# Row 0 five weight groups ahead of row 1 instead of four, 40 attention pieces beside row 1's units, SBUF tiles at 2 KB boundaries

## The chip, the cores and the metric

The kernel runs on one core of a Trainium2 chip. A core has five engines that run beside each other, each through its own list of instructions in order: TensorE (PE, matrix products), VectorE (DVE), ScalarE (ACT), GpSimd (POOL) and SyncE (SP, which here issues all transfers). They meet at semaphores. SBUF is the on-chip memory, 128 partitions wide; products land in PSUM. The metric is the device time of one launch in microseconds (us); lower is better.

## The reference

Two transformer layers on an input of 2 rows x 512 positions x 512 channels. Each layer has an attention and a feed-forward part, each behind a layer norm with shift, scale and gate that come from a conditioning vector per row:

```python
sa, ca, ga, sb, cb, gb = (silu(c) @ wmod) ...      # per row of the batch
x = x + ga * L0_attn(layernorm(x) * (1 + ca) + sa)
x = x + gb * L0_ffn(layernorm(x) * (1 + cb) + sb)   # weights reduced to their sign
x = x + ga' * L1_attn(layernorm(x) * (1 + ca') + sa')
x = x + gb' * L1_ffn(layernorm(x) * (1 + cb') + sb')
```

- Layer 0's attention is a gated linear recurrence: 32 heads of 128 channels, 8 key/value groups of 4 heads, computed in 4 chunks of 128 positions with a state carried from chunk to chunk, a decay per head, an RMS norm, a gate and an output projection.
- Layer 0's feed-forward is one 512 x 512 product with sign weights.
- Layer 1's attention is softmax attention with 32 heads of 16 channels over 512 positions of a row.
- Layer 1's feed-forward mixes 4 streams of 128 channels; the 4 x 4 mixing matrix of each position comes from 50 Sinkhorn iterations, a long chain of tiny operations.

The two rows of the batch do not depend on each other anywhere.

## The kernel before

**Units of layer 0.** The work of layer 0's attention is cut into *steps*, one for each pair of a weight group (0 to 7) and a row (0 or 1), and each step into 4 *units*, one for each chunk of 128 positions: 16 steps, 64 units. `AHEAD` sets the order of the steps. The first `8 - AHEAD` groups are done for row 0 and row 1 by turns, so that the weights of a group are loaded once for both rows; then row 0 does its last `AHEAD` groups alone, and then row 1 does its own. The weights of these last groups are loaded twice, once for each row. With `AHEAD = 4`, units 0 to 31 alternate, units 32 to 47 are row 0's, units 48 to 63 are row 1's.

```python
    steps = [(g, b) for g in range(KV0 - AHEAD) for b in range(B)]
    steps += [(g, b) for b in range(B) for g in range(KV0 - AHEAD, KV0)]
```

A group of weights is 14 tiles of 128 x 512 numbers (256 KB): 1 for the keys, 4 for the queries, 1 for the values, 4 for the gate, 4 for the output. Each is loaded by SyncE (`raw_tile`, line 200), split into a high part by ACT (line 209) and a low part by POOL (line 210), since each product is made of three passes over such parts (`passes`, line 232). The loop over units (from line 1374) issues, beside the unit's own work, the projections and the loads of the next steps.

A unit has the scores (`scores`, decays loaded as `gb` at line 493), the state, `mix` (its first products into `yps`, line 548, are used here as the start of a unit), the turn of its result and the output projection into `x` (`project_out`).

**The tail of a row.** `tail(n)` is called after unit n. For each row it runs, chunk by chunk over the next units, the layer norm, the feed-forward of layer 0 (products at line 629), the second layer norm, and at last the projections of layer 1's keys, values and queries. `ends` says at which unit a row's tail begins: the second chunk of its last step, 45 for row 0 and 61 for row 1. The projections follow 8 units later, at unit 53 for row 0. They go through a bias on ACT (line 661), a rotation on VectorE and POOL (lines 668 to 671), a split (lines 673 and 675), are stored to DRAM (line 678) and loaded again in another shape (lines 797 and 808), all through SyncE's one queue.

**Pieces of layer 1's attention.** The softmax attention is cut into 128 *pieces*, 64 for each row. `piece()` issues, for piece p, two score tiles of 128 x 512 (product at line 842) with their maxima on VectorE (line 846), and, ten pieces later, the transposed scores (line 876) with the exponentials on ACT; every fourth piece also the output of one set of heads (line 896). Pieces begin beside row 1's units: from unit `FIRST` on, `PER = 3` pieces are issued after each unit, up to `HOLD` pieces in all:

```python
        while n >= FIRST and at[0] < min(HOLD, (n - FIRST + 1) * PER):
            piece()
```

With `FIRST = 53` and `HOLD = 33` these are 33 pieces over units 53 to 63. After the last unit the rest follow. The steps of row 1's tail that are still open then (12 virtual units) are taken one per piece from piece `HOLD` on; row 1's own pieces are 64 to 127. The Sinkhorn chains are put beside the pieces (`aside`), row 0's on POOL for the most part, row 1's on VectorE; the last one remains alone at the end.

**What sets the order.** The program is traced in the order of these calls, and a scheduler then orders each engine's instructions by priorities and its own view of when data is there; `gated` and `behind` add order-only links so that side work keeps its place. The tile pools share one SBUF space: each tile gets its address after scheduling, wherever it fits among the tiles that live at the same time. Before the change most 2 KB tiles start 128, 640 or 1,152 bytes past a 2 KB boundary.

Of the kernel before, what the change touches and what calls it, by code (L numbers as in the profile page):

```python
# [12 lines left out]
PT, OUT = 16, 1  # L13
S1, S2, MT, OT, OP = 3, 3, 2, 2, 2
QS = 6
HOLD = 33
UPS = 400, 400, 400, 400
RATES = None, None, None, None
HEAD = 16
# [4 lines left out]
HL, RA, ZL, XC, XP = 0, 0, 100, 100, 1  # L24
UPO = 600
SPLIT0, SPLIT1 = 16, 16
AHEAD = 4
FIRST = 53
PER = 3
LATE, LATE1 = 2, 12  # L30
LAG = 10
# [21 lines left out]
def tile_adaln(ctx: ExitStack, tc: tile.TileContext, a: dict, out: bass.AP):  # L53
    nc = tc.nc
    ck = ctx.enter_context(tc.tile_pool(name="ck", bufs=1))
    raws = ctx.enter_context(tc.tile_pool(name="raw", bufs=RAW))
    wts = ctx.enter_context(tc.tile_pool(name="w", bufs=1))
    small = ctx.enter_context(tc.tile_pool(name="small", bufs=4))
    wk = ctx.enter_context(tc.tile_pool(name="wk", bufs=2))
    dram = ctx.enter_context(tc.tile_pool(name="dram", bufs=1, space=bass.MemoryType.DRAM))  # L60
    psp = ctx.enter_context(tc.tile_pool(name="ps", bufs=2, space=PSUM))


    table = nc.scalar.preload_act_table_set("natural_log_exp_and_others")
# [583 lines left out]
    def load_rope1():  # L648
        l1c["rope"] = [temp([P, L], FP, f"rope1{k}", 1) for k in range(2)]
        for k in range(2):  # L650
            nc.sync.dma_start(out=l1c["rope"][k], in_=a["c_rope1"][:, k * L:(k + 1) * L])
        if "bias" not in l1c:
            l1c["bias"] = keep([P, 6])
            nc.sync.dma_start(out=l1c["bias"], in_=a["bias1"])
# [33 lines left out]

    ends = [(KV0 - AHEAD) * B * NC + AHEAD * NC - NC + 1, KV0 * B * NC - NC + 1]

    def tail(n):

        if n % 8 in (3, 4, 5, 6) and n < 40:
            mod_piece(load=n % 8 < 6)

        for b in range(B):
            c = n - ends[b]
            with behind():
                if -3 <= c < 1:
                    load_ffn(c + 3)  # L700
                    if c == -2:
                        load_ffn_rows(b)
                elif c == 5:
                    load_l1(b)
                elif 6 <= c < 8:
                    load_l1q(2 * c - 12)
                    load_l1q(2 * c - 11)
                    if c == 7:
                        load_rope1()
                if n == FIRST - 1:  # L710
                    layer1_keys()
            if 0 <= c < NC:
                l1c["a", c] = norm(x[b * NC + c])
            if 1 <= c < NC + 1:
                modulated(b, c - 1, l1c["a", c - 1], modT[0], 2, also=sum_h)
                l1c["sums", c - 1] = l1c["sum"]
            if 2 <= c < NC + 2:
                feed_forward(b, c - 2)
            if 3 <= c < NC + 3:
                l1c["b", c - 3] = norm(x[b * NC + c - 3])  # L720
            if 4 <= c < NC + 4:
                modulated(b, c - 4, l1c["b", c - 4], modT[1], 0)
            if c == 8:
                l1c["there", b] = True
                project_kv(b)
                project_q(b, 0)
                project_q(b, 1)
                project_q(b, 2)
                project_q(b, 3)
# [10 lines left out]
    def layer1_keys(js=(0, 1)):  # L740
        for s in range(2):
            empty = temp([P, L], FR, "hi1")
            nc.scalar.copy(empty, raw_tile(a["c_keys1"][s]))
            for j in js:
                ksd[j, s] = temp([P, L], FR, f"ks{j}{s}")
                nc.sync.dma_start(out=ksd[j, s].bitcast(FP), in_=empty.bitcast(FP))

    steps = [(g, b) for g in range(KV0 - AHEAD) for b in range(B)]
    steps += [(g, b) for b in range(B) for g in range(KV0 - AHEAD, KV0)]
    units = [{"at": (g, b, c)} for g, b in steps for c in range(NC)]  # L750
# [534 lines left out]
    def slack(p):  # L1285

        return LAG0 if p < HOLD else min(LAG, LAG0 + p - HOLD)

    def piece():
        p = at[0]  # L1290
        at[0] += 1
        if p == 0:
            begin()
        i, k = divmod(p, 8)
        if k == 0 and i < len(order):
            load_step(i + 1)
        if p < n_pieces:
            maxima(order[i], k)
        if wt[0] <= p - slack(p):
            weighed()  # L1300
        if k == 4 and i + 1 < len(order):
            keys1(i + 1)
        with tc.high_priority(UP):
            if p >= HOLD and p % POP == 0 and virtual:
                tail(virtual.pop(0))
        aside(2)
# [67 lines left out]
    for n, u in enumerate(units):  # L1374
# [39 lines left out]
        with extra(n):  # L1414
            tail(n)
        while n >= FIRST and at[0] < min(HOLD, (n - FIRST + 1) * PER):
            piece()
# [86 lines left out]
```

## Time and profile before

| | |
|---|---|
| median of 3 runs | 1406.62 us (1404.83 to 1407.78) |
| the profiled execution | 1401.8 us, span 1400.0 us |
| busy, TensorE / VectorE / ACT / POOL | 1245.7 / 1159.8 / 831.5 / 775.8 us |
| mean granted TensorE clock | 0.948 |
| read from HBM / written | 102.11 / 10.64 MB |
| unit 0, unit 63 (first product into `yps`) | 87.9 us, 1015.8 us |
| first score tile of row 0, of row 1 | 897.1 us, 1129.2 us |
| last transposed scores | 1270.2 us |

The span is the time from the first to the last instruction; the profiled execution's own time is 1.8 us more. Busy time of an engine counts its instructions, not its waits. A line such as `a:b d, PE busy (x) ...` gives, for the stretch from a to b, its length, and for each engine the busy time and the number of instructions, then the granted share of TensorE's clock, the share of time the transfer engines were busy and the bytes they moved.

Four phases can be told apart: the start up to about 100 us, layer 0's attention of both rows up to about 1020 us (in its last third row 0's tail and the first pieces run beside it), the pieces up to 1272 us, and the rest of row 1's Sinkhorn chain and mixing up to 1400 us.

### The profile page before, as it was taken

Reading aid. Unit: us, or ns where it says so; the run is one execution under the profiler, and the core shown is the slowest. Engines: PE = TensorE matmul, PEld = TensorE weight load, DVE = VectorE, ACT = ScalarE, POOL = GpSimd, SP = SyncE. Lnnn points to the kernel's source line nnn. Section 1 sums busy time; section 2 is a strip of 40 time slices with the busy share of each in tenths; the row PEclk is TensorE's granted clock in tenths of the full one; section 3 lists DMA queues with packets and bytes.
Section 4 is the critical chain, followed back from the end, with each engine's and each line's share of the span. In section 5 each row is a group of like instructions: output and inputs, shape, how many; then the busy total and the mean of one; then the engine's idle time right before and its main releaser. Section 6 shows DMA issues by size and latency. Waiting matters only on the chain. (4 is left out here: it accounts for less than half of the span.)

```text
span 1400.0 us, 22901 instructions
## 1 busy us (share of the span) xinstructions
PE 1245.7 (89%) x7168; PEld 992.1 (71%) x7168; DVE 1159.8 (83%) x2969; ACT 831.5 (59%) x2354; POOL 775.8 (55%) x1169
## 2 busy tenths in 40 slices
PE   5979999999999999999988999799999889994128
PEld 3758888788788778888866777577676666663117
DVE  7998668687677687787899977688799979898887
ACT  5457576476376466666665656557567467664128
POOL 4454374364264367577777748545242655558861
PEclk9989999999999999999999999999999999997568
DMA  8022241231142343324333317523203231200001
GB/s 256 23 65 60 88 121 30 68 107 53 53 118 57 92 120 106 98 68 124 118 114 91 98 53 241 170 67 91 90 24 113 71 111 52 59 11 1 1 16 46
DMA packets 95377, 117.13 MB, mean 84 GB/s; under 512 B 10828, under 2 KB 50508, under 8 KB 95256
## 3 DMA queue, kind: packets, MB, share of 16 engines
q1 hardware_dynamic: 95256, 115.67, 27.7%
q8 instruction: 57, 0.93, 0.3%
q14 instruction: 64, 0.52, 0.1%
HBM read 102.11 MB, written 10.64 MB: 81 GB/s over the span
## 5 line engine op out<-in xcount | busy, mean ns | idle before, releaser
L846 DVE TENSOR_REDUCE m<-s 128x1 f32<-128x512 f32 x256 | 166.4, 673 | 18.6 <-PE s L842 18.3
L67 ACT ACTIVATE pt<-s 128x512 f32<-128x512 f32 x256 | 136.9, 602 | 33.3 <-PE s L876 31.7
L447 POOL TENSOR_TENSOR q<-xcos,rot 128x512 f32<-128x512 f32 x64 | 92.8, 1450 | 61.6 <-DVE xcos L445 57.1
L67 ACT ACTIVATE sg<-sg 128x512 f32<-128x512 f32 x128 | 80.6, 632 | 68.5 <-DVE sg L478 66.8
L876 PE MATMUL s<-qs,ks 100*128 100x256 f32 x512 | 103.3, 306 | 11.0 <-DMA qs<-mm 7.4
L842 PE MATMUL s<-ks,qs 96*128 96x512 f32 x256 | 103.6, 437 | 9.7 <-DVE m L846 7.5
L515 POOL TENSOR_TENSOR gb<-gb,q 128x512 f32<-128x512 f32 x48 | 63.2, 1319 | 77.7 <-ACT gb L67 68.7
L232 PE MATMUL pps<-hh,wq_h 128*128 128x512 f32 x256 | 103.2, 403 | 1.7 <-ACT vT L766 1.1
L876 PEld LDWEIGHTS s<-qs,ks 100*128 100x128 f32 x512 | 80.9, 195 | 33.5 <-ACT pt L67 8.9
L232 PE MATMUL gps<-wg_h,hh 128*128 128x512 f32 x256 | 101.8, 400 | 2.9 <-ACT wg_h L209 2.7
L232 PE MATMUL ops<-wo_h,zh 128*128 128x512 f32 x256 | 101.5, 397 | 1.7 <-ACT zh L570 1.0
L232 PE MATMUL ops<-wo_h,zl 128*128 128x512 f32 x256 | 100.8, 394 | 0.7 <-DVE zl L571 0.7
L232 PE MATMUL pps<-hl,wq_h 128*128 128x512 f32 x256 | 101.3, 396 | 0.0
L232 PE MATMUL pps<-hh,wq_l 128*128 128x512 f32 x256 | 101.2, 395 | 0.0
L232 PE MATMUL gps<-wg_l,hh 128*128 128x512 f32 x256 | 101.2, 395 | 0.0
L232 PE MATMUL gps<-wg_h,hl 128*128 128x512 f32 x256 | 100.6, 393 | 0.0
L232 PE MATMUL ops<-wo_l,zh 128*128 128x512 f32 x256 | 99.9, 390 | 0.0
L67 ACT ACTIVATE dec<-dec,room 128x128 f32<-128x128 f32 x256 | 83.0, 398 | 21.8 <-POOL dec L495 21.7
L548 PE MATMUL yps<-v,dec 128*128 128x128 f32 x512 | 94.2, 280 | 1.8 <-DVE xcos L445 1.0
L495 POOL TENSOR_SCALAR_AFFINE_SELECT dec<-gb 128x512 f32<-128x512 f32 x64 | 49.1, 768 | 80.7 <-DMA gb<-g_dram 51.8
L522 POOL TENSOR_TENSOR xw<-v,room 128x512 f32<-128x512 f32 x48 | 55.2, 1163 | 68.5 <-ACT v L462 64.3
L558 DVE SCALAR_TENSOR_TENSOR z<-yps,ss,sg 128x128 f32<-128x128 f32 x256 | 71.9, 340 | 24.0 <-ACT ss L67 23.8
(323 smaller groups left out, 3968.5 us busy)
## 6 DMA issues: line engine op xcount, KB each, us to landing
gb<-g_dram SPq DMA_DIRECT2D x64, 256.0 KB
raw<-in_wq SPq DMA_DIRECT2D x56, 256.0 KB
raw<-in_wg SPq DMA_DIRECT2D x48, 256.0 KB
raw<-in_wo SPq DMA_DIRECT2D x48, 256.0 KB
raw<-in_wmod SPq DMA_DIRECT2D x40, 256.0 KB
qs<-q_dram SPq DMA_DIRECT2D x64, 96.0 KB
q_dram<-hi SPq DMA_DIRECT2D x16, 256.0 KB
raw<-in_wk SPq DMA_DIRECT2D x14, 256.0 KB
```

What stands on the lines that cost most here:

```text
L67: ins = nc.scalar.activation(o, i, func, **kw)
L232: nc.tensor.matmul(ps, lhsT=l, rhs=r, start=i == 0, stop=i == n - 1)
L447: nc.gpsimd.tensor_tensor(dst, sp(xc_), sp(rot), ALU.add)
L495: anchor["pool"] = nc.gpsimd.affine_select(out=dec, in_=gb, pattern=[[0, REP0], [1, P]], compare_op=ALU.is_ge, fill=-1e30, base=0, channel ...
L515: nc.gpsimd.tensor_tensor(gb, gb, q[:, c], ALU.mult)
L522: nc.gpsimd.tensor_tensor(xw, u["v"][:, c, :].unsqueeze(1).to_broadcast(sh4), wdc[:, c, r0:r0 + REP0].unsqueeze(2).to_broadcast(sh4), ALU. ...
L548: nc.tensor.matmul(yps[:, h, :], lhsT=u["pr"][:, h, :], rhs=u["v"][:, c, :], start=True, stop=not c)
L558: nc.vector.scalar_tensor_tensor(z[:, h, :], yps[:, h, :], ss[:, h:h + 1], sg[:, h * P:(h + 1) * P], ALU.mult, ALU.mult)
L842: anchor["pe"] = nc.tensor.matmul(ps, lhsT=st["qs"][rp][0:KS, i, qt * P:(qt + 1) * P], rhs=st["ks"][s][0:KS], start=True, stop=True,).ins
L846: anchor["dve"] = nc.vector.tensor_reduce(st["m"][:, 2 * qt + s, i:i + 1], ps, AX.X, ALU.max, negate=True).ins
L876: nc.tensor.matmul(ps[:, j, :], lhsT=st["ks"][s][0:KM, kt * P:(kt + 1) * P], rhs=st["qs"][rp][0:KM, i, :], start=True, stop=True,)
```

## The change

`AHEAD` goes from 4 to 5: units 0 to 23 alternate, units 24 to 43 are row 0's, units 44 to 63 are row 1's. Row 0's tail begins after unit 41 instead of 45, and its projections stand at unit 49 instead of 53. One more group of weights is loaded twice. `FIRST` goes from 53 to 49 and `HOLD` from 33 to 40: 40 pieces stand beside row 1's units 49 to 62, and 24 of row 0's pieces are left after the last unit instead of 31. The pools `ck`, `raw`, `w` and `wk` are wrapped so that each tile whose row is a whole multiple of 2 KB starts at a 2 KB boundary.

```diff
-HOLD = 33
+HOLD = 40
...
-AHEAD = 4
-FIRST = 53
+AHEAD = 5
+FIRST = 49
...
+    class Aligned:
+
+        def __init__(self, pool):
+            self.pool = pool
+
+        def tile(self, shape, dt, **kw):
+            whole = int(np.prod(shape[1:])) * 4 % 2048 == 0
+            return self.pool.tile(shape, dt, **kw, **({"align_bytes": 2048} if whole else {}))
+
+    ck, raws, wts, wk = Aligned(ck), Aligned(raws), Aligned(wts), Aligned(wk)
```

## The prediction

> **What bounds the kernel now.** I read the page's slices first, for where TensorE is not full, then the busy time of each engine in stretches cut at the starts of row units (the first product into `yps`, line 548) and of layer 1's score tiles (line 842), then the waits of the last stretch.
>
> ```profile
> span 1400.0 us, 22901 instructions
> PE   5979999999999999999988999799999889994128
> DVE  7998668687677687787899977688799979898887
> PEclk9989999999999999999999999999999999997568
> ```
>
> TensorE is full from slice 4 to slice 20, has holes from slice 21 (700 us) to slice 33, and is idle in the last four, where row 1's stream mixing runs on VectorE.
>
> ```profile
> core 0: us, PE busy (x) PEld busy (x) DVE busy (x) ACT busy (x) POOL busy (x), PEclk, DMA share, GB/s
> 341.60:505.90 164.30, 164.30 (x846) 132.25 (x845) 119.72 (x249) 93.62 (x276) 75.66 (x63) 1.00 0.27 79
> 616.80:668.70 51.90, 51.90 (x270) 44.13 (x269) 42.88 (x84) 35.13 (x101) 37.42 (x31) 1.00 0.36 107
> 668.70:900.40 231.70, 208.33 (x1010) 170.39 (x1009) 198.29 (x371) 134.99 (x384) 161.98 (x131) 0.97 0.43 131
> 900.40:1003.20 102.80, 96.42 (x573) 74.93 (x571) 90.00 (x190) 66.06 (x183) 42.25 (x39) 0.95 0.26 79
> 1003.20:1087.70 84.50, 80.45 (x590) 60.57 (x586) 77.22 (x203) 57.01 (x158) 30.93 (x41) 0.98 0.20 63
> 1087.70:1129.20 41.50, 37.29 (x237) 27.15 (x238) 37.71 (x93) 20.95 (x51) 27.15 (x35) 0.92 0.34 103
> 1129.20:1272.00 142.80, 132.23 (x1175) 93.68 (x1177) 122.83 (x443) 97.87 (x234) 81.29 (x313) 0.98 0.16 45
> 1272.00:1400.00 128.00, 46.00 (x316) 43.11 (x308) 109.51 (x570) 50.35 (x180) 73.99 (x318) 0.66 0.05 17
> ```
>
> The rows are: units 20 to 31; units 40 to 43; units 44 to 55 (row 0's feed-forward and projections run beside row 1's units; call it the handover); units 56 to 61 with pieces of attention; from there to row 1's first layer-1 projection; from that projection to row 1's first score tile; the rest of the attention; the stream mixing alone. TensorE bounds all but the last. What can be won is its idle time: 231.7 - 208.3 = 23.4 us in the handover, 6.4, 4.1, 4.2 and 10.6 us behind it. The change adds no product, so it gains only where it closes such holes and loses where it opens one.
>
> **The change part by part.** Sums go against the profiled execution, 1401.8 us with a span of 1400.0; the median of the runs is 1406.62, 4.8 us above it. A difference in the span is added to the median. I cost each engine's order in the two built programs by the trace: every instruction at its group's busy time over its count (a projection product 0.23 us, a score product 0.28, and so on).
>
> *One more group loaded twice.* The count of weight loads goes from 12 groups to 13: 14 more transfers of 256 KB, 14 more copies on ACT (line 209, 0.62 us, 8.6 us) and 14 more subtractions on POOL (line 210, 1.30 us, 18.1 us). The new loads fall into units 20 to 31. SyncE's queue passes them between the `gb` loads of line 493. There TensorE is busy 164.3 of 164.3 us, VectorE 73%, POOL 46%, DMA 27%, so they are covered. At units 32 to 35, where the kernel before begins to load a group per step, TensorE lost 1.8 us. Bounds 0 to 2; I take 0.8.
>
> ```profile
> L454 DVE TENSOR_TENSOR ql<-q,qh x64: 668/1014/1784, 64.3 to 972.9; 128x512 fp32r<-128x512 f32 x64
> ```
>
> This subtraction takes 0.67 us or up to 1.78 us. [...]
>
> *The handover, four units earlier.* It moves from units 44 to 55 to units 40 to 51. TensorE's order there is 94% the same, its work 206.8 us against 203.4, VectorE's 181.9 against 182.5. The same stretch, so the same time plus the work: 231.7 + 3.4 = 235.1 us. The holes are moved, not closed.
>
> *Ten units beside pieces instead of six.* Units 52 to 61 hold 166.1 us of TensorE work against 93.7 before in units 56 to 61. That work came from units 40 to 43 (no idle at all) and from the tail. The old stretch was idle 6.4 of 102.8 us (6.2%); VectorE's share of the work falls from 0.85 to 0.82, which speaks for less; the next row's share is 4.8%. At 5.5%: 166.1 / 0.945 = 175.8 us. Bounds: the idle share of units 100 us to 700 us, 0.55%, gives 167.0; the whole stretch with its slow-clock time, 102.8 / 93.7, gives 182.2.
>
> *Row 1's tail with 24 pieces of row 0 left, not 31.* From unit 62 to row 1's first projection: TensorE 77.6 against 81.4 us, VectorE 81.8 against 86.0. VectorE carries it: 84.5 x 159.4 / 167.4 = 80.5 us.
>
> *From row 1's first projection to its first score tile.* Before, the order between them has 72 projection products, 19 + 30 score products and three output runs: 35.8 us. After, it has the 72 products, 24 score products, and no score tile of line 842 at all: row 0's are used up, and 23.2 us of TensorE work and 19.5 us of VectorE work are left. The wait that takes over is row 1's first queries. They go through the bias, the rotation, the split, a store and a load:
>
> ```profile
> 1103.28 0.69 ACT L661 ACTIVATE raw<-pps,room 128x512 f32<-128x512 f32 x1 [0.88 <-POOL lo L675]
> 1117.80 1.53 SPq L678 DMA_DIRECT2D q_dram<-lo  x1
> 1120.49 2.60 SPq L808 DMA_DIRECT2D qs<-q_dram  x4
> ```
>
> From bias to load issue 17.2 us here, 24.7 us for row 0 (844.88 to 869.61). In the new order the third projection ends 10.4 us after the first begins, and 12.7 us of work follow it. So the score tile waits to 10.4 + 17.2 + 2 (the landing, from the 1.9 us by which `qs` loads hold the chain) = 29.6 us; with row 0's pace 37; with an undisturbed path (0.69 bias, 0.74 shuffle, 1.8 and 1.8 rotation, 0.62 and 1.3 split, 3 for the second projection that stands ahead in SyncE's queue, 2.7 store, 2 load) 25. I take 30, nearest to row 1's own pace. The products behind that score tile on TensorE, and everything behind its maximum on VectorE, wait with it.
>
> *Behind it.* The orders are equal to within 1 us from row 1's ninth score piece on. 5.7 us of TensorE work now stands ahead of the first score tile instead of behind it; that stretch took 18.0 us and loses 4.2: 270.8 - 4.2 = 266.6 us.
>
> *Alignment.* It moves addresses, and with them little of the order (137 of 5934 products when taken alone). Lined up with the built program's addresses, line 558 takes 338 to 344 ns for each of its four places, the one that crosses a 2 KB boundary included (340). No tile before is aligned, so a gain or loss is bounded only by that: 3 ns of 340 on the PE-bound path, 3 us either way. I take 0.
>
> Sum from 616.8 us: 0.8 + 235.1 + 175.8 + 80.5 + 30 + 266.6 = 788.8, against 783.2 (51.9 + 231.7 + 102.8 + 84.5 + 41.5 + 270.8). The span grows by 5.6 us; the median goes to 1412.2.
>
> ```profile
> 861.83 0.50 PE L232 MATMUL cps<-xwl,kth 128*128 128x512 f32 x1 [2.06 <-DVE xwl L454]
> 863.57 0.63 PE L232 MATMUL pps<-hl,wq_h 128*128 128x512 f32 x1
> ```
>
> A hole of 2.06 us on TensorE was followed by half the clock (in the profile's record of the granted clock 0.5 for 3.4 us): products of 0.63 us, not 0.39. [...]
>
> **The rivals.** *Faster.* The wait for row 1's queries is short, since no maxima stand in VectorE's way any more, and the ten units run as full as units before 700 us. Then 175.8 becomes 167.0 and 30 becomes 25: 5.6 - 8.8 - 5.0 = -8.2, 1398.4 us. For it: VectorE's lower share. Against: the old stretch with pieces was idle 6.2%. It decides from the point where the idle share of units 52 to 61 falls below 2.4% with the wait as taken. *No change.* One of the two comes true by half: about 1406.6. *Much slower.* Row 0's pace holds for row 1 (37 us), the ten units lose as much as the six did with their slow clock (182.2), and each of two holes brings a slow window (3.4 us at half rate, 1.7 us each): 5.6 + 7 + 6.4 + 3.4 = 22.4, 1429 us. *The change does not do what it says:* row 0's pieces could start no earlier because its projections are late. The built order speaks against that: its first score tile stands 52 us of TensorE work earlier.
>
> **How the numbers follow.** The forecast (3 to 15 us slower) 0.46, much slower 0.10, no change 0.18, faster 0.26. A measurement here tells about 0.2% (2.8 us) from no change. Range: from 1400, which leaves out the faster rival's far end (0.1), to 1424 (0.08 above); the forecast's own range is 1409.5 to 1421.5.
>
> **What would show it.** Right: the first score tile of row 1 preceded by a TensorE wait of 5 us or more; no such wait in units 40 to 43 beyond the moved handover; 23 us idle in the handover at units 40 to 51. Wrong: TensorE over 97% busy in units 52 to 61, no wait at row 1's first score tile, or a changed duration of one and the same instruction by its new address.

## The result, and the profile after

The changed kernel takes 1418.41 us (median of 4 runs, 1416.31 to 1422.14) against 1405.72 us (1400.54 to 1407.78) for the kernel before on the same chip: 1.0116 times as long, with a 95% interval of 1.0085 to 1.0146. The profiled execution took 1419.15 us with a span of 1417.3 us, 17.3 us more than before; the sum had said 5.6 us. By the medians the loss is 12.7 us: the profiled execution of the kernel before, 1401.8 us, was 3.9 us faster than its median, so the two traces overstate it. Lines of the changed kernel lie 11 further down: 842 is now 853, 876 is 887, 232 is 243.

The page's head and slices of the changed kernel, in the same form as before:

```profile
span 1417.3 us, 23045 instructions
PE   6989999999999999999989979999999969994038
DVE  7998668677677786798998578867789979898887
PEclk9999999999999999999999999999999989997569
```

Slices 21 to 32 now hold two below 9 (8 and 7), where there were four (8, 8, 7 and 8): the holes in the middle are fewer. But the 33rd slice (1134 to 1169 us) falls from 8 to 6. The busy time of each engine in stretches, now cut exactly where the terms of the sum begin and end (the columns are those of the windows shown of before):

```profile
core 0: us, PE busy (x) PEld busy (x) DVE busy (x) ACT busy (x) POOL busy (x), PEclk, DMA share, GB/s
620.70:853.50 232.80, 212.71 (x1023) 173.60 (x1021) 198.49 (x377) 136.98 (x388) 164.24 (x132) 0.96 0.44 132
853.50:1035.90 182.40, 171.50 (x1011) 133.99 (x1011) 143.84 (x301) 115.47 (x310) 80.61 (x72) 0.94 0.26 77
1035.90:1114.50 78.60, 75.28 (x568) 58.84 (x564) 73.82 (x200) 53.32 (x150) 31.16 (x42) 0.98 0.15 48
1114.50:1149.60 35.10, 22.55 (x114) 18.47 (x115) 28.45 (x65) 18.89 (x46) 25.87 (x29) 0.93 0.34 107
1149.60:1285.20 135.60, 127.47 (x1114) 87.73 (x1117) 119.76 (x423) 87.83 (x212) 75.55 (x300) 0.97 0.17 50
1285.20:1417.30 132.10, 49.84 (x333) 46.16 (x332) 111.51 (x586) 52.46 (x184) 77.45 (x333) 0.68 0.04 17
```

The rows are: the handover, units 40 to 51; units 52 to 61 beside pieces; from unit 62 to row 1's first projection; from there to row 1's first score tile; to the last transposed scores; the mixing alone. In the fourth row TensorE is busy for 22.55 of 35.10 us. Three views of that place follow. TensorE's longest waits between 1085 and 1290 us (columns: total, times, longest):

```profile
PE s L853 <- ACT pt L78: 10.2, 1, 10.2
PE s L887 <- DMA qs<-mm: 7.3, 11, 1.3
```

TensorE's timeline there (start, duration, instruction, and in brackets the idle time before it):

```profile
1138.82 0.60 PE L833 MATMUL vps<-room,vT 128*128 128x128 f32 x4
1149.62 2.94 PE L853 MATMUL s<-ks,qs 96*128 96x512 f32 x5 [10.20 <-ACT pt L78]
```

The queries that this score tile waits for, in the timelines of ACT (their bias) and of SyncE (the last of their stores, and the loads of line 819, with other rows left out at the dots):

```profile
1127.56 0.68 ACT L672 ACTIVATE raw<-pps,room 128x512 f32<-128x512 f32 x1
...
1139.52 0.57 SPq L689 DMA_DIRECT2D q_dram<-lo  x1
...
1143.57 5.51 SPq L819 DMA_DIRECT2D qs<-q_dram  x6
```

From 1139.4 us on the next product in TensorE's list is row 1's first score tile. It reads the first two of the six loads, issued at 1143.57 and 1143.93 us; by their semaphores in the trace these had landed at 1148.66 and 1149.37 us, and the tile starts 0.25 us after the second. The view names ACT as the releaser, and ACT was late too:

```profile
1143.81 0.62 ACT L684 CAST hi<-raw 128x512 fp32r<-128x512 f32 x1 [3.64 <-DVE raw L682]
1147.31 0.62 ACT L684 CAST hi<-raw 128x512 fp32r<-128x512 f32 x1 [2.88 <-DVE raw L682]
1147.83 1.56 ACT L78 ACTIVATE pt<-s 128x512 f32<-128x512 f32 x3
```

The three exponentials of row 0's last transposed scores stood in ACT's list behind two casts of later query projections, which waited for VectorE. The tile waits for ACT's semaphore as well, and the trace does not tell for which of the three. So without the late queries ACT might have held it until some point between 1148.4 and 1149.4 us, and the 10.2 us are not shown to be the queries' alone. In the three kernels below with the same wait the tile starts 0.14 us after its queries have landed, and the view puts the wait down to `qs<-q_dram`. The clock then falls, in the windows of the wait and of what comes right behind it:

```profile
1139.42:1149.60 10.18, 0.00 (x1) 0.01 (x1) 6.56 (x10) 3.45 (x7) 9.01 (x14) 0.74 0.54 173
1149.60:1153.00 3.40, 3.38 (x6) 1.68 (x6) 2.58 (x5) 0.00 (x0) 0.12 (x1) 0.50 0.57 149
```

The granted clock is 0.50 and six products take 3.38 us. The trace's record of the clock has it at half for 13.7 us from 1144.3 us.

A whole-stretch view makes the kernels comparable: from unit 20 to the last transposed scores each does the same work on TensorE (some 5,227 products in each trace), so the length of the stretch is its busy time (which half clock lengthens: a projection product takes 0.63 us at a granted clock of 0.50 at 863.6 us of the kernel before, and 0.39 us at full clock at 866.2 us) plus its idle time. The kernel before:

```profile
341.60:1270.20 928.60, 878.66 (x5227) 694.08 (x5229) 775.60 (x1788) 578.52 (x1592) 534.22 (x707) 0.98 0.31 91
```

and the changed kernel:

```profile
344.40:1285.20 940.80, 883.40 (x5227) 697.15 (x5228) 777.78 (x1779) 587.32 (x1604) 552.34 (x713) 0.97 0.31 94
```

Idle time goes from 49.9 to 57.4 us (+7.5), and the same products take 4.7 us longer. Of the 17.3 us of the span these are 12.2; 2.8 us are there before unit 20, where the loads of the changed kernel do not differ yet, and 2.3 us behind the last transposed scores. Unit 20 starts between 341.6 and 345.1 us in all kernels below, with no relation to their time, so I put those 2.8 us down to the spread between executions. Such a table compares single executions: on one and the same chip those of the kernel before ran from 1395.45 to 1409.13 us, so a difference of 2 or 3 us between two traces need not come from the kernel.

### The profile page after: what moved, and what is told of

The parts are those of the page before. It is cut to its first block, busy times and chain, and to the rows that moved or that the text cites. A ratio compares the mean times of both kernels' runs of the same rounds, so it can differ in the third digit from the quotient of the medians.

```text
span 1417.3 us, 23045 instructions
## 1 busy us (share of the span) xinstructions
PE 1254.1 (88%) x7168; PEld 998.8 (70%) x7168; DVE 1161.7 (82%) x2969; ACT 840.7 (59%) x2368; POOL 794.2 (56%) x1183
## 4 chain that ended last, share of the span: by engine, by line
PE 50%; DVE 24%; POOL 9%; ACT 6%; DMA 6%; issue 4%; SPq 0%; POOLq 0%; DVEq 0%; ACTq 0%
PE pps L243 11%; PE ops L243 8%; PE gps L243 7%; PE op L907 3%; PE s L887 3%; PE s L853 3%; PE yps L559 3%; DVE m L857 2%; PE mix L1193 2%; PE sps L243 2%; PE yps L561 2%; DVE ql L465 2%; POOL q L458 2%; DMA qs<-mm 2%; PE cps L243 1%
## 5 line engine op out<-in xcount | busy, mean ns | idle before, releaser
L857 DVE TENSOR_REDUCE m<-s 128x1 f32<-128x512 f32 x256 | 166.1, 672 | 18.9 <-PE s L853 18.6
L853 PE MATMUL s<-ks,qs 96*128 96x512 f32 x256 | 105.0, 449 | 17.9 <-ACT pt L78 10.2
L559 PEld LDWEIGHTS yps<-v,dec 128*128 128x128 f32 x512 | 80.6, 197 | 13.8 <-issue 5.1
```

What stands on the lines that cost most here:

```text
L559: nc.tensor.matmul(yps[:, h, :], lhsT=u["pr"][:, h, :], rhs=u["v"][:, c, :], start=True, stop=not c)
L853: anchor["pe"] = nc.tensor.matmul(ps, lhsT=st["qs"][rp][0:KS, i, qt * P:(qt + 1) * P], rhs=st["ks"][s][0:KS], start=True, stop=True,).ins
L857: anchor["dve"] = nc.vector.tensor_reduce(st["m"][:, 2 * qt + s, i:i + 1], ps, AX.X, ALU.max, negate=True).ins
```

## The experiments

Twelve kernels, each timed against the kernel before, with the ratio's 95% interval. Every kernel but the one before has the aligned pools; "align" has nothing else changed. The last three columns are from each kernel's trace: TensorE's idle and busy time from unit 20 to the last transposed scores, and the longest wait of TensorE at row 1's first score tile.

| kernel | groups ahead, pieces beside units | median us | ratio | idle us | busy us | wait us |
|---|---|---|---|---|---|---|
| before | 4, 33 | 1405.72 | 1 | 49.9 | 878.7 | 0 |
| changed | 5, 40 | 1418.41 | 1.0116 [1.0085, 1.0146] | 57.4 | 883.4 | 10.2 |
| e1_align | 4, 33, align | 1404.54 | 1.0002 [0.9986, 1.0019] | 48.1 | 876.5 | 0 |
| e2_hold28 | 5, 28 | 1404.41 | 1.0007 [0.9988, 1.0027] | 46.3 | 883.0 | 0 |
| e3_first53 | 5, 33 from unit 53 | 1415.10 | 1.0077 [1.0050, 1.0104] | 52.4 | 884.2 | 0 |
| e4_a4_40 | 4, 40 | 1417.46 | 1.0097 [1.0070, 1.0124] | 58.3 | 884.0 | 6.2 |
| e5_hold33 | 5, 33 | 1420.45 | 1.0129 [1.0109, 1.0148] | 56.9 | 889.6 | 7.0 |
| e6_vlast | 5, 40, values last | 1426.70 | 1.0170 [1.0152, 1.0189] | 61.5 | 886.5 | 4.4 |
| e7_a5_per2 | 5, 28, two per unit | 1406.80 | 1.0028 [1.0013, 1.0042] | 48.2 | 878.5 | 0 |
| e8_a4_per2 | 4, 22, two per unit | 1403.00 | 1.0004 [0.9984, 1.0025] | 46.7 | 878.7 | 0 |
| e9_a5_other_q | 5, 40, other queries | 1419.98 | 1.0125 [1.0095, 1.0154] | 54.0 | 889.1 | 0 |
| e10_a4_other_q | 4, 33, other queries | 1403.74 | 1.0009 [0.9988, 1.0029] | 48.8 | 879.2 | 0 |
| e11_hold24 | 5, 24 | 1405.02 | 1.0008 [0.9989, 1.0027] | 47.9 | 881.1 | 0 |
| e12_a4_hold28 | 4, 28 | 1406.05 | 1.0021 [1.0004, 1.0039] | 47.4 | 882.2 | 0 |

The kernels fall into two groups. Eight, before among them, are within 0.3% of it and idle 46.3 to 49.9 us in the stretch; six take 0.8% to 1.7% longer and idle 52.4 to 61.5 us. Busy time tells them apart only just: 876.5 to 883.0 us in the eight, 883.4 us or more in the six.

**The alignment alone.** To the kernel before only the wrapped pools are added:

```diff
+    ck, raws, wts, wk = Aligned(ck), Aligned(raws), Aligned(wts), Aligned(wk)
```

> The kernel before with the 2 KB alignment alone; the order of row 0 and the pieces as before. Theory (the time is lost at row 1's first score tile and in the longer stretch with pieces): the same as before within 3 us, and single instructions as long as before. Rival (the new addresses cost the time): 8 us or more slower, with longer instructions of the same kind.

Measured 1.0002 [0.9986, 1.0019]. The instruction whose durations by address the prediction went by, line 558 before and line 569 here, in the view of its tile (min/median/max in ns):

```profile
L569 DVE SCALAR_TENSOR_TENSOR z<-yps,ss,sg x256: 319/342/353, 99.8 to 1021.7; 128x128 f32<-128x128 f32 x128
```

Before, the same instruction took 310/340/352 ns. Alignment is free, and the loss lies elsewhere.

**Fewer pieces beside the units, five groups ahead.** 28 instead of 40, later 24:

```diff
-HOLD = 40
+HOLD = 28
```

> The changed kernel with 28 pieces beside row 1's units instead of 40. The built order then has 15 of row 0's score products between row 1's first projection and its first score tile, where the changed kernel has none, and 19.6 us of TensorE work behind the third projection instead of 12.7. Theory: the wait of 10.2 us at row 1's first score tile falls to 4 us or less and the kernel takes 8 to 12 us less than the changed one, 3 to 8 us more than before. Rival (the fifth group's second load and the earlier handover cost it): as slow as the changed kernel, 12 us or more over before.

> The changed kernel with 24 pieces beside row 1's units. The built order has 18 of row 0's score products between row 1's first projection and its first score tile and 22.3 us of TensorE work behind the third projection. Theory (from 28 pieces on downwards nothing is left to win): within 3 us of before, as with 28. Rival (each piece beside the units costs): 2 to 4 us faster than with 28.

Measured 1.0007 [0.9988, 1.0027] and 1.0008 [0.9989, 1.0027]. The whole stretch of the second:

```profile
342.70:1271.70 929.00, 881.13 (x5227) 693.72 (x5229) 777.23 (x1780) 585.90 (x1604) 550.06 (x716) 0.98 0.31 95
```

Idle time is 47.9 us, and there is no wait at row 1's first score tile. With 28 pieces even the 3 to 8 us over before that the theory had left did not show (1.0 us). Both kernels keep the fifth group, its 14 more loads and the whole move of the handover. So with 28 or 24 pieces these cost nothing that can be measured, and gain nothing either; the loss of the changed kernel came with the 12 pieces more beside the units. In the built orders 15 and 18 of row 0's score products (line 853) stand between row 1's first projection and its first score tile, 19 before and none in the changed kernel: this is the work that covers the queries' round trip.

**Forty pieces with four groups ahead.** The kernel before, aligned, with more pieces per unit:

```diff
-HOLD = 33
+HOLD = 40
...
-PER = 3
+PER = 4
```

> Row 0 four groups ahead as before, tiles aligned, 40 pieces beside row 1's units by taking four after each unit from unit 53. The built order has none of row 0's score products between row 1's first projection and its first score tile, and 11.0 us of TensorE work behind the third projection. Theory: the wait at row 1's first score tile appears here too, 8 to 14 us, and the kernel is 6 to 14 us slower than before though no group is loaded a second time. Rival (the fifth group costs it): the same as before within 3 us.

Measured 1.0097 [1.0070, 1.0124]. TensorE's longest wait around row 1's first score tile:

```profile
PE s L853 <- DMA qs<-q_dram: 6.2, 1, 6.2
```

The same wait, here put down to the queries' load itself. It is shorter than the 8 to 14 us expected, while the time, 13.6 us over before, is as expected. Five groups ahead are not needed for the loss; forty pieces, four after each unit, are enough.

**Thirty-three pieces, five groups.** `HOLD` from 40 to 33, and then the same with `FIRST` back at 53:

```diff
-HOLD = 40
+HOLD = 33
...
-FIRST = 49
+FIRST = 53
```

> The changed kernel with 33 pieces beside row 1's units, which lies between the 28 (ratio 1.0007) and the 40 (1.0116). The built order has 10 of row 0's score products between row 1's first projection and its first score tile and 16.6 us of TensorE work behind the third projection (12.7 with 40, 19.6 with 28). Theory (the wait for row 1's first queries is the round trip less the work in front): TensorE idle between first projection and first score tile about 9 us (12.6 with 40, 5.7 with 28), the kernel 4 to 9 us over before. Rival (it is the number of pieces beside the units that costs, through holes in the units): the wait as with 28, the loss in units 56 to 63.

> The changed kernel with row 0 five groups ahead and aligned tiles, but pieces from unit 53 on and 33 of them, as before. Theory: no wait of more than 4 us at row 1's first score tile (18 of row 0's score products stand before it, 23.3 us of TensorE work behind the third projection); within 4 us of before. Rival (the fifth group costs it): 12 us or more over before.

Measured 1.0129 [1.0109, 1.0148] with `HOLD` alone and 1.0077 [1.0050, 1.0104] with both. With `HOLD` alone, TensorE's longest wait there, and behind it the stretch from row 1's first score tile to its ninth piece:

```profile
PE s L853 <- DMA qs<-q_dram: 7.0, 1, 7.0
```

and in the windows:

```profile
1141.40:1162.80 21.40, 19.01 (x117) 12.59 (x118) 12.25 (x31) 9.18 (x19) 6.89 (x23) 0.67 0.37 112
```

Seven pieces fewer beside the units did not bring the cover back: by the built orders, costed as in the prediction, 12.7 us of TensorE work stand between the third projection and the score tile in the changed kernel, 16.6 us here, 22.5 before and 19.6 with 28 pieces. TensorE was idle for 9.8 us between row 1's first projection and its first score tile, as the theory had it (about 9). But the kernel is 18.1 us over before, where 4 to 9 were expected, so that idle time is not the whole loss. The granted clock in the 21.4 us behind the wait is 0.67. This kernel has the most half-clock time of all, 71.7 us in the whole stretch against 41.0 before.

With `FIRST` at 53 there is no wait at the score tile (23.3 us of work stand behind the third projection), and yet the kernel is 0.8% longer. Its whole stretch, and under it that of the kernel with alignment alone, from which it differs in `AHEAD` and nothing else:

```profile
342.60:1279.20 936.60, 884.16 (x5227) 698.46 (x5229) 775.70 (x1786) 584.93 (x1605) 551.25 (x722) 0.97 0.31 94
345.10:1269.70 924.60, 876.53 (x5227) 696.29 (x5229) 773.76 (x1786) 577.81 (x1591) 534.36 (x708) 0.98 0.30 91
```

So with 33 pieces from unit 53 the fifth group does cost time: 1.0077 against 1.0002. The expectation, within 4 us of before, failed at 10.8 us, and the rival's 12 us lie inside the interval (7.0 to 14.6). Of the 8.0 us by which the stretch is longer than before, 2.5 are idle time and 5.5 are products that take longer; the clock is at half for 61.4 us. One hole of 6.1 us at 834.0 us, in the handover, is followed by 10.2 us of half clock; but with alignment alone there is also a hole of 6.1 us (888.7 us, 6.8 us of half clock behind it), and that kernel takes no longer than before (1.0002). So the wait at row 1's tile is not the only way to lose: this kernel loses without it, mostly by the clock. Why the fifth group makes the holes fall worse here, and not with 28 or 24 pieces, isn't settled.

**The queue behind the round trip.** Row 1's projections are stored in the order values, keys, queries. Here the values are projected and stored last:

```diff
-        nc.sync.dma_start(out=v_dram[b], in_=biased("wv1", 0, 5, b))
+        if b == 0:
+            nc.sync.dma_start(out=v_dram[b], in_=biased("wv1", 0, 5, b))
...
+                if b:
+                    nc.sync.dma_start(out=v_dram[b], in_=biased("wv1", 0, 5, b))
```

> The changed kernel with row 1's value projection moved behind its query projections, so that the first queries are projected second instead of third. The built order has 48 of the 72 projection products before row 1's first score tile. Theory (a round trip of fixed length from the first queries' projection sets that tile): from row 1's first projection to its first score tile 31 to 33 us instead of 35.1, still with a wait of 8 us or more, and the kernel 2 to 5 us faster than the changed one. Rival (TensorE work in front of the tile sets it): shorter by the 24 products' 5.6 us and no wait left.

Measured 1.0170 [1.0152, 1.0189], by the ratios another 0.5% longer than the changed kernel. TensorE's longest waits there:

```profile
PE vps L836 <- DMA vT<-v_dram: 6.1, 1, 6.1
PE s L856 <- DMA qs<-q_dram: 4.4, 1, 4.4
```

The score tile did come earlier: 28.9 us after the first projection instead of 35.1, and its wait fell from 10.2 to 4.4 us. The values now came late, for 6.1 us. The two waits together are as long as the one before. So the theory failed: the tile came 2 to 4 us earlier than it said, with half the wait, and the kernel is slower where it had 2 to 5 us faster. The rival named the shorter way (5.6 us, 6.2 measured), but not the wait that is left.

**The round trip taken out for the first pieces.** Row 1's first eight pieces read row 0's keys and queries, which have long been stored, so they do other numbers with the same work:

```diff
-            nc.sync.dma_start(out=order[i]["ks"][s].bitcast(FP)[48 * s:48 * s + 48], in_=k_dram[b][2 * t + s])
+            nc.sync.dma_start(out=order[i]["ks"][s].bitcast(FP)[48 * s:48 * s + 48], in_=k_dram[0 if i == 8 else b][2 * t + s])
...
-                    in_=q_dram[b][h:h + 2, :, half * Q:half * Q + Q].rearrange("r k q -> k r q"),
+                    in_=q_dram[0 if i == 8 else b][h:h + 2, :, half * Q:half * Q + Q].rearrange("r k q -> k r q"),
```

> The changed kernel, but the queries and keys of row 1's first eight pieces are loaded from row 0's store, which was written long before; the work stays the same, the result of these eight pieces does not. So the round trip of row 1's first queries no longer stands before row 1's first score tile. Theory (that wait costs about 8 us of the loss): no wait over 3 us there, and the kernel 6 to 10 us faster than the changed one, still 4 to 10 us over before, because the slow-clock windows beside the pieces remain. Rival (the wait is only the place where a loss from elsewhere shows): within 3 us of the changed kernel.

> The same replacement of the loads of row 1's first eight pieces, in the kernel before with aligned tiles. Theory: there is no such wait in it, so within 3 us of before. Rival (the loads from another row are cheaper by themselves): 5 us or more faster than before.

With four groups and 33 pieces: 1.0009 [0.9988, 1.0029]; there was no wait to take away. With the changed kernel's settings: 1.0125 [1.0095, 1.0154], as slow as the changed kernel, as its rival had it, where the theory of one late tile had it 6 to 10 us faster. Row 1's first score tile now starts 0.6 us after the first projection and waits for nothing. TensorE's longest wait between 1080 and 1165 us is now another:

```profile
PE s L887 <- DMA qs<-mm: 5.7, 2, 5.0
```

It is for the row maxima of an earlier piece. The view of their tile (count, duration, first and last start) has them copied by ACT at 1152.3 us:

```profile
L872 ACT CAST mm<-mt x1: 358/358/358, 1152.3 to 1152.3; 8x256 fp32r<-8x256 f32 x1
```

SyncE's timeline behind that:

```profile
1154.47 0.78 SPq L819 DMA_DIRECT2D qs<-q_dram  x2
1155.35 0.37 SPq L808 DMA_DIRECT2D ks<-k_dram  x1
1155.82 0.58 SPq L689 DMA_DIRECT2D q_dram<-hi  x1
1156.51 0.68 SPq L873 DMA_DIRECT2D qs<-mm  x1
```

And the waits of SyncE's queue in the same stretch:

```profile
SPq L819 <- DMA q_dram<-lo: 11.0, 2, 6.0
```

The maxima are ready at 1152.7 us and leave at 1156.5, since they stand in SyncE's one queue behind the loads of the next pieces' queries, which wait up to 6.0 us for the true store. The wait for the round trip was moved from the tile to the queue, and it holds TensorE from there. Shorter by half, it did not give the time back: idle time is 3.4 us less than in the changed kernel, but the same products take 5.7 us more (889.1 against 883.4). Half clock does not explain that: during products it lasts 48.8 us, 48.3 in the changed kernel. Most of the 5.7 us lie in the output products of line 907: the same 996 of them are busy for 68.6 us against 63.0, and between 1131.7 and 1136.2 us they stand in runs of 2 to 6 among projection products, 0.62 us a run, where a run of 32 takes 1.93 us. Whether that broken order is why the time did not come back isn't shown; the kernel with 28 pieces has 66.3 us there and loses nothing.

**Two pieces per unit, and 28 with four groups.** `PER` 3 to 2 (with `HOLD` 28 and 22), and `HOLD` 33 to 28:

```diff
-PER = 3
+PER = 2
```

> The changed kernel with two pieces after each unit instead of three, from unit 49 on, 28 in all. The built order has 25 of row 0's score products between row 1's first projection and its first score tile and 29.5 us of TensorE work behind the third projection. Theory: no wait at that tile, idle 4 us or less in that stretch, and fewer holes beside the units since VectorE has less to do there: 1 to 4 us faster than with 28 pieces at three per unit, so 0 to 3 us faster than before. Rival: pieces taken out of the units leave holes there, 3 us or more over before.

> Row 0 four groups ahead as before, tiles aligned, two pieces after each unit from unit 53 on, 22 in all instead of 33. The built order has 41 of row 0's score products between row 1's first projection and its first score tile. Theory: no wait there; the units are emptier of VectorE work, the tail fuller; within 3 us of before. Rival (more of row 0's pieces behind the last unit is simply better): 4 us or more faster than before.

> Row 0 four groups ahead as before, tiles aligned, 28 pieces beside row 1's units instead of 33. Theory: within 3 us of before, since 33 with four groups leave 19 score products in front of row 1's first score tile already. Rival (fewer pieces beside the units spare slow-clock windows): 4 us or more faster than before.

Measured 1.0028 [1.0013, 1.0042] with five groups, 1.0004 [0.9984, 1.0025] with four, and 1.0021 [1.0004, 1.0039]. The first is 3.9 us over before, where its theory had 0 to 3 us faster and its rival 3 us or more slower; the holes that the rival named do not show, since the whole stretch takes 926.7 us in its trace against 928.6. The other two are within 3 us, as expected. With 25, 41 and 18 of row 0's score products between row 1's first projection and its first score tile, none has the wait. None is faster than before either: more cover than the round trip needs was worth nothing here. No kernel of this study beats the kernel before by more than its interval.

## Why the prediction was right and where it was not

The direction was right, the time lies inside the range (1400 to 1424, and in the likeliest case's own 1409.5 to 1421.5), and the wait that was to take over came where it was said. But the middle of the forecast, 5.6 us, is less than half of the 12.7 us measured, and the two terms that decide it were 6.6 and 5.1 us too short; that the time still lies in the likeliest case's range is owed in part to the width of that range. Term by term, from the same marks:

| term | predicted us | measured us |
|---|---|---|
| start of unit 40 | 616.8 + 0.8 | 620.7 |
| handover, units 40 to 51 | 235.1 | 232.8 |
| ten units beside pieces | 175.8 (167.0 to 182.2) | 182.4 |
| unit 62 to row 1's first projection | 80.5 | 78.6 |
| to row 1's first score tile | 30 (25 to 37) | 35.1 |
| to the end | 266.6 | 267.7 |

- **One more group loaded twice: right up to unit 40, and not in general.** The loss before unit 40 is 3.1 us more than taken, but 2.8 us of that are there before unit 20. The kernels with 28 and 24 pieces keep all 14 loads and end at 1.0007 and 1.0008. The subtraction of line 465 (454 before), whose row the prediction shows, has a median of 990 ns against 1014 before, and of 692 against 688 in units 20 to 31. But with 33 pieces from unit 53 the fifth group costs 0.75%, behind unit 40 (1.0077 against 1.0002); no term had such a cost.
- **The handover: right.** It was moved, not closed: 20.1 us idle against 23.4.
- **The ten units: at the upper bound.** This is the largest miss, 6.6 us. Idle time was 10.9 us, and 9.7 were taken, so the idle share of 5.5% was nearly right (6.0%). The products were what failed: 166.1 us of work, counted at each group's mean, took 171.5 us at a granted clock of 0.94. In these ten units half clock lasted 19.0 us during products. The prediction's sum has no term for the slower clock here, and this was wrong.
- **From row 1's first projection to its first score tile: the mechanism right, the size 5.1 us short.** The parts as put: 10.4 to the queries' bias, 17.2 from bias to load issue, 2 for the landing. Measured: 13.1, 16.0 and 6.0. From bias to load issue the path was well read from row 1's own pace. The landing was mis-sized: in the chain of the kernel before, the 1.9 us are those of `qs<-mm`, the 8 KB of maxima, and not of the queries' loads of 96 KB. The first two of these landed 5.1 and 5.4 us after their issue by the trace's semaphores, and 5.1 and 4.9 us in the kernel before, where nothing waited for them. In four of the other kernels the second of them took 2.0 to 2.2 us, so 2 us is possible, but it is not what the trace at hand showed. Another 2.7 us lie ahead of the bias, which ACT began 1.9 us after the third projection had ended.
- **Behind it: right**, to 1.1 us, and **the tail**, to 1.9, though not because VectorE carries it: TensorE was busy for 75.3 of the 78.6 us and VectorE for 73.8.
- **Alignment: right.** 1.0002.

The forecast had said what would show it wrong: TensorE more than 97% busy in units 52 to 61 (94.0% measured), no wait at row 1's first score tile (10.2 us), a changed duration by address (none). Of its rivals, "faster" fell by the first two, and "much slower" had the right extra mechanism, half clock behind holes, but counted two windows of 1.7 us. In the whole stretch, half clock during products went from 40.3 to 48.3 us, by my estimate some 4 us of time (half of the 8.0 us more), and the busy time grew by 4.7 us.

The changed kernel's trace has eleven records of half clock in the whole stretch, nine of them behind holes of 1.4 us and more (the two longest holes are of 4.2 and 10.2 us).

What is shown and what is argued: that the changed kernel's loss comes with its 40 pieces, and not with the fifth group's loads or the alignment alone, is shown (28 and 24 pieces with five groups lose nothing, alignment alone loses nothing, and 40 pieces with four groups lose 1.0%). That the fifth group is free at any number of pieces is not so: 33 pieces lose nothing with four groups and 0.8% to 1.3% with five. Whether the number counts or how many follow each unit is not separated with four groups, since the 40 there come four at a time. That TensorE waits for the queries' round trip where too few of row 0's pieces are left in front of row 1's first score tile (10 or none) is shown in four kernels. That this wait alone is the whole loss is not: with other queries it is gone from the tile and the time stays, and 33 pieces from unit 53 lose 0.8% without it. The rest goes with half clock behind holes (61.4 us of half clock with 33 pieces from unit 53, 41.0 us before), and what sets where these fall stays open.

## What to carry to other kernels

Work that is free to move can be needed where something with a long latency has to be covered, here a store and load through one queue (22.1 us from the bias of row 1's first queries to the score tile in the changed kernel); before such work is brought forward, count how much of it is left at that place against the measured round trip. A wait that is taken away at one instruction may stand in the queue behind it, as it did here, where it held 8 KB of maxima for 3.8 us, so look next at what else goes through that queue. And a bounding engine's busy time summed from means fell short here: the ten units, with holes of 1.7, 1.4 and 2.1 us (899.2, 937.2 and 981.9 us) and 19.0 us of half clock during products, took 171.5 us for work counted at 166.1. Price the half clock that the traces at hand show behind such holes. Settings that are free one by one can cost together: here the fifth group with 28 pieces, and 33 pieces with four groups, lost nothing, and both together 0.8%.

## What was not expected of the hardware

- Half clock came behind short holes too, and for different lengths of time: in the changed kernel holes of 2.1 us (981.9 us) and 3.3 us (740.5 us) were followed by 6.8 us of it each, and in the one of 10.2 us (1139.4 us) a stretch of 13.7 us in one piece began. Not behind every hole: three of 1.2 to 1.6 us in the changed kernel (696.7, 1210.6 and 1249.2 us), and one of 3.1 us in the kernel before (710.7 us), were followed by none.
- Two pieces of data that have nothing to do with each other were tied by SyncE's queue: 8 KB of maxima, ready, waited 3.8 us behind loads that waited for a store.
- One and the same load, the second of row 1's first queries (96 KB), took 2.0 to 2.2 us from issue to landing in four kernels and 4.4 to 5.8 us in eight.
- Addresses of tiles in SBUF, aligned to 2 KB or not, made no difference to the time (1.0002 with the alignment alone) and hardly any to the VectorE instruction of line 569 (319 to 353 ns aligned, 310 to 352 before).
